# Column-tiled projections, router products and scores, and padded FFN weights, in a two-layer transformer kernel

## The chip, the core and the metric

The kernel runs on one core of a Trainium2 chip. A core has five engines with queues of their own: TensorE (matrix products; the profile splits it into PE, the products, and PEld, the loads of the stationary operand), VectorE (DVE), ScalarE (ACT), GpSimd (POOL) and SyncE (SP), which here issues DMAs. The metric is the device time of one execution in microseconds, lower is better. The unit of work is one call on a batch of 8 sequences of 512 tokens, each token 512 wide, in fp32.

## What is computed

The reference chains two post-norm layers. Cut to what matters here:

```python
# layer 0: 16 heads of 32, causal; then 8 experts, the best 2 of each token
x = layernorm(x + attn0(x))            # q, k, v = x @ W.T + b; softmax(q k^T / sqrt(32)) v; out @ WO.T + b
x = layernorm(x + moe(x))              # softmax router with LoRA, top 2, gate-up, silu, down, LoRA on both
# layer 1: 8 query heads of 64, 2 key/value heads, no mask; then a quantised FFN
x = layernorm(x + attn1(x))            # h = norm_scale * x / (norm + eps) * split_scale; x + out @ Wo.T
x = layernorm(x + ffn(x))              # W = (wq - 128) * scale; silu(x Wg^T) * (x Wu^T), then @ Wd^T; hidden 1408
```

## The kernel before

The program is one pass over four stages. In the profiled execution layer 0 attention takes the first 700 us or so, the experts run to about 1133 us, layer 1 attention to 1677 us and the FFN to the end.

**Layer 0 attention** (`attention0`) works a batch (one sequence) at a time, and in it four groups of four heads. A group's queries and keys are kept transposed: 4 heads x 32 features on the 128 partitions, 512 tokens along the row. `query` (L1301) and `key` (L1313) make them as four accumulated products of 128 x 128 weights by 128 x 512 inputs; `value` (L1294) and `project` (L1321) are products of the same size. `scores` (L1386) multiplies, for a block of 128 keys, the four heads' keys by the queries from that block on. A head has 32 features, so each of the four products uses 32 rows of the array and all 128 columns, and each writes its own PSUM bank. Key blocks come in three units: block 0 (512 queries), blocks 1 and 3 (384 and 128), block 2 (256). ACT then takes the exponential, POOL masks the diagonal block (L1395), and `product` (L1410) multiplies the values of each head (32 columns) by the probabilities, into a quarter of the partitions each. `normalise` (L1425) sums the probabilities with a matrix of ones, 32 columns a head, and DVE inverts and multiplies.

`plan` fills the slots: a slot is one unit of scores, then the projections or router products that are due in it, then the `product` of the unit before, and in every third slot a `normalise`. In the middle of this stage the framework's scheduler sets the order on each engine; at its start, in the last half of the last batch and afterwards the order is that of the source (`in_order`).

**The router** (`Router`) works beside the attention of later batches: `logits` (L491), `choose` (L503: four products of 128 tokens by 8 experts), `dispatch` (L547 and L548: ranks of the tokens within each expert, by products with a triangle and with ones) and `enter` (L588: 16 bf16 products of one-hot rows that write the table of tokens of each expert). LoRA products (`delta`, L781: 16 rows by 128 columns) are merged into the experts' weights in the same stage.

**Layer 1 attention** (`Attention1`) is planned by hand for every engine. Its products go through `multiply` (L1600), which issues each of them as a pair of 64-column halves, except for some of batch 0. `score` (L1745) multiplies 64-row keys by queries for two heads at a time, with all 128 columns; `product` (L1767) and the sums (L1775) use 64 columns a head.

**The FFN** (`IntegerFfn`) splits inputs and hidden values into a high and a low fp32r half. Of each batch, `hidden` (L1152) makes 11 blocks of 128 hidden features: 8 products for the gate (ps_g) and 8 for the up part (ps_u) with the integer weights as the stationary operand, and `out` (L1168) 8 products of the hidden halves with the down weights as the moving operand. The weights are held in two tiles: the first 20 units (gate and up of blocks 0 to 9) in a pool `c_weights` that is opened before layer 1 attention, the other 13 (all down weights, and gate and up of block 10) in `d_weights`, opened with the FFN. The pool `c_weights` lies on the right side of the memory, below the rows of batches 2 to 7, so what is in it sets the byte at which its first tile starts.

The lines of before that the change touches most:

```python
def multiply(self, b, out, lhsT, rhs, c):                       # layer 1
    for m in (slice(0, self.HD), slice(self.HD, P)) if b else (slice(0, P),):
        self.nc.tensor.matmul(out[m], lhsT=lhsT[:, m], rhs=rhs, start=c == 0, stop=c == ND - 1)
```

Of the kernel before, what the change touches and what calls it, by code (L numbers as in the profile page):

```python
# [54 lines left out]
N_VEC = 16 + 2 * NHID  # L55

# [360 lines left out]
class Router:  # L417
# [76 lines left out]
    def choose(self, b, parts, ps):  # L494
# [7 lines left out]
        for t in range(NT):  # L502
            nc.tensor.matmul(ps[:, t, :], lhsT=parts[:, ts(t, P)], rhs=self.gather, start=True, stop=True)  # L503
# [39 lines left out]
    def dispatch(self, b, ps):  # L543

        nc, small = self.nc, self.small
        flat = "p t e -> p (t e)"
        nc.tensor.matmul(ps.rearrange(flat), lhsT=self.before, rhs=self.both.rearrange(flat), start=True, stop=False)  # L547
        nc.tensor.matmul(ps.rearrange(flat), lhsT=self.ones, rhs=self.earlier.rearrange(flat), start=False, stop=True)  # L548
        here = slice(NT * b, NT * (b + 1))
        parts = small.tile([P, TOP_K, NT], F32, name="parts")  # L550
        for k in range(TOP_K):
            for of_expert, out in ((ps, self.ranks[:, k, here]), (self.part, parts[:, k, :])):
                mine = small.tile([P, NT, E], F32, name="mine")
                nc.vector.tensor_tensor(mine, of_expert, self.hots[:, k, here, :], ALU.mult)
                nc.vector.tensor_reduce(out, mine, AX.X, ALU.add)
# [27 lines left out]
    def enter(self, ps, low, high, column):  # L583

        nc, n = self.nc, TOP_K * NT
        for h, part in enumerate((low, high)):
            for i in range(n):
                nc.tensor.matmul(ps[:, h, :], lhsT=part[:, i, :], rhs=column[:, i, :], start=i == 0, stop=i == n - 1)  # L588
        nc.vector.tensor_tensor(self.table, ps[:, 0, :], self.table, ALU.add)
        nc.vector.scalar_tensor_tensor(self.table, ps[:, 1, :], float(P), self.table, ALU.mult, ALU.add)  # L590
# [632 lines left out]
def attention0(env, guard, keep, routes, experts, dram, p_mm, tiles_ctx):  # L1223
# [8 lines left out]
    with ExitStack() as phase:  # L1232
# [57 lines left out]

        def value(b, t):
            ps = mm([P, D], "ps_v")
            for c in range(ND):
                nc.tensor.matmul(ps, lhsT=xts[b][:, c, ts(t, P)], rhs=wv[:, c, :], start=c == 0, stop=c == ND - 1)  # L1294
            vs[t] = own.tile([P, D], F32, tag=f"v{t}", name=f"v{t}")
            nc.vector.tensor_tensor(vs[t], ps, row[:, 0, :], ALU.add)

        def query(b, g):
            ps = mm([P, S], "ps_q")
            for c in range(ND):  # L1300
                nc.tensor.matmul(ps, lhsT=wq[:, g, ts(c, P)], rhs=xts[b][:, c, :], start=c == 0, stop=c == ND - 1)  # L1301
# [8 lines left out]
        def key(b, g):  # L1310
            ps = mm([P, S], "ps_k")
            for c in range(ND):
                nc.tensor.matmul(ps, lhsT=wk[:, g, ts(c, P)], rhs=xts[b][:, c, :], start=c == 0, stop=c == ND - 1)  # L1313
# [4 lines left out]
        def project(b, t):  # L1318
            ps = mm([P, D], "ps_o")
            for c in range(ND):  # L1320
                nc.tensor.matmul(ps, lhsT=aoTs[b][:, c, ts(t, P)], rhs=wo[:, c, :], start=c == 0, stop=c == ND - 1)  # L1321
# [40 lines left out]
        def choose(b):  # L1362
            router.choose(b, logits.pop(b), mm([P, NT, E], "ps_r"))

        def dispatch(b, mm=mm):
            router.dispatch(b, mm([P, NT, E], "ps_rank"))
# [8 lines left out]
        def enter(rows, mm=mm):  # L1375
            router.enter(mm([P, 2, E * E_TILES], "ps_table"), *rows)

        def scores(b, g, u):
# [3 lines left out]
            for kt in UNITS[u]:  # L1382
                w = S - P * kt
                for j in range(4):
                    hs = slice(HD * j, HD * (j + 1))
                    nc.tensor.matmul(sc[:, j, width : width + w], lhsT=k[hs, ts(kt, P)], rhs=q[hs, P * kt :],  # L1386
                                     start=True, stop=True)
# [157 lines left out]
        project(b, 0)  # L1545
        project(b, 1)
        rows = one_hot(b - 1, (2, 3))
        project(b, 2)
        project(b, 3)
        experts.load(7)  # L1550
        enter(rows)
# [8 lines left out]
        choose(b)  # L1560
        tiles.step()
        merge()
        dispatch(b, tiles.aside)
# [4 lines left out]
        enter(rows, tiles.aside)  # L1568
# [8 lines left out]
class Attention1:  # L1577
# [19 lines left out]
    def multiply(self, b, out, lhsT, rhs, c):  # L1597

        for m in (slice(0, self.HD), slice(self.HD, P)) if b else (slice(0, P),):
            self.nc.tensor.matmul(out[m], lhsT=lhsT[:, m], rhs=rhs, start=c == 0, stop=c == ND - 1)  # L1600
# [87 lines left out]
    def batches(self, work, p_sc, p_av, weights, split):  # L1688
# [51 lines left out]
        def score(b, g, kt):  # L1740
            st = state[b]
            sc = p_sc.tile([P, 2, S], F32, tag="sc", name="sc1")
            for j in range(2):
                hs = slice(HD * j, HD * (j + 1))
                nc.tensor.matmul(sc[:, j, :], lhsT=st["kT"][hs, ts(kt, P)], rhs=st["qT"][g][hs, :],  # L1745
                                 start=True, stop=True)
# [121 lines left out]
def usual_pass(tc, ins, held_out):  # L1868
    nc = tc.nc
    with ExitStack() as ctx:  # L1870
# [4 lines left out]
        with tc.tile_pool(name="a_mm", bufs=2, space=PSUM) as p_mm, ExitStack() as attn1_ctx:  # L1875
# [29 lines left out]
            weights.open(ctx.enter_context(tc.tile_pool(name="c_weights", bufs=1, side="right")), weights.FIRST)  # L1905
# [309 lines left out]
```

## Time and profile before

| What | us |
|---|---|
| median of 3 runs | 2182.87 (2181.64 to 2183.12) |
| the profiled execution | 2183.3 |
| its span, first instruction to last | 2181.6 |
| TensorE drawn busy (PE) | 2151.6, 99% of the span |
| VectorE busy | 1273.8, 58% |
| ScalarE busy | 627.5, 29% |
| GpSimd busy | 497.8, 23% |

The costliest TensorE groups, from the page's list of groups of instructions (busy time of the group, mean length of one instruction):

| group | instructions | busy us | mean ns |
|---|---|---|---|
| L1168 ps_f, FFN out | 672 | 170.3 | 393 |
| L1152 ps_g and ps_u, FFN hidden, four groups | 352 each | 138.6 to 139.0 each | 394 to 395 |
| L1745 layer 1 scores, 64 rows x 128 columns | 512 | 127.2 | 615 |
| L1301, L1313, L1294, L1321 layer 0 projections, 128 x 128 | 256 each | 115.9 to 120.7 each | 598 to 613 |

In the profile's lines a TensorE form such as 32*128 is rows*columns of the array that the stationary operand fills, and 128x512 is partitions x elements of the moving operand. An fp32 product of the source appears as two instructions. Lengths of single matmuls overlap[...]; the distance from one start to the next is what a matmul costs.

### The profile page before, as it was taken

The page shows a single profiled execution, that of the slowest core. Times are in us where ns is not written, and L with a number is a line of the kernel's source. Part 1 is how long each engine was busy: PE and PEld are TensorE (multiplying, and loading weights), DVE is VectorE, ACT ScalarE, POOL GpSimd, SP SyncE. Part 2 cuts the span into 40 slices and gives each one's busy share as a digit, 9 for nine tenths or more (in the row PEclk, how much of TensorE's full clock was granted, in tenths as well). Part 3 has the DMA queues.
Part 4 walks back from the last instruction along what each step waited for, and adds up shares of the span by engine and source line. Part 5 has one row for each costly group of instructions (what it writes and reads, how often), then busy time and mean ns, then how long its engine had stood idle before and what let it go on. Part 6 is the DMA issues. An engine that isn't in the chain of part 4 may idle for free. (4 is left out here: it accounts for less than half of the span.)

```text
span 2181.6 us, 25149 instructions
## 1 busy us (share of the span) xinstructions
PE 2151.6 (99%) x9694; PEld 1077.7 (49%) x9694; DVE 1273.8 (58%) x2042; ACT 627.5 (29%) x907; POOL 497.8 (23%) x489
## 2 busy tenths in 40 slices
PE   9999999999999999999999999999999999999997
PEld 3334444444444444444443333333334888888876
DVE  3557665675758543324316988889857644555443
ACT  2332323323223231122123333333332232222222
POOL 2332414324233442132015122231211000000000
PEclk9999999999999999999999999999999999999999
DMA  8030302303132328787644121331201311111000
GB/s 304 20 94 4 97 20 78 97 1 97 33 102 78 107 67 232 212 228 207 192 142 157 49 87 58 97 97 39 78 1 44 102 59 58 58 58 58 20 20 21
DMA packets 159971, 194.87 MB, mean 89 GB/s; under 512 B 61011, under 2 KB 101971, under 8 KB 157283
## 3 DMA queue, kind: packets, MB, share of 16 engines
q1 hardware_dynamic: 148560, 157.49, 23.5%
q0 software_dynamic: 10560, 34.61, 5.5%
q8 instruction: 79, 1.29, 0.2%
q10 hardware_dynamic: 722, 1.07, 0.1%
q14 instruction: 50, 0.40, 0.1%
HBM read 123.67 MB, written 69.47 MB: 89 GB/s over the span
## 5 line engine op out<-in xcount | busy, mean ns | idle before, releaser
L903 PE MATMUL ps_gu<-experts,xrT 128*128 128x512 f32 (+1 forms) x520 | 247.2, 598 | 0.0
L1390 ACT ACTIVATE p<-sc 128x2048 f32<-128x2048 f32 (+1 forms) x96 | 152.9, 1592 | 162.2 <-PE sc L1386 135.8
L1157 DVE SCALAR_TENSOR_TENSOR hT<-ps_u,vec,sg 128x512 f32<-128x512 f32 x88 | 65.6, 745 | 194.6 <-PE ps_u L1152 194.6
L1395 POOL TENSOR_SCALAR_AFFINE_SELECT p<-p 128x512 f32<-128x512 f32 x128 | 92.4, 734 | 360.3 <-ACT p L1390 316.8
L1168 PE MATMUL ps_f<-ffn_w,h_half 128*128 128x512 f32 x672 | 170.3, 393 | 0.6 <-issue 0.4
L1007 POOL TENSOR_TENSOR g_total<-g_total,r_inv 128x512 f32<-128x512 f32 x64 | 89.6, 1400 | 343.7 <-DVE r_inv L1778 272.2
L1418 DVE TENSOR_TENSOR p<-p 128x1536 f32<-128x1536 f32 (+2 forms) x96 | 131.1, 1365 | 46.0 <-POOL p L1395 41.0
L1748 ACT ACTIVATE p<-sc 128x1024 f32<-128x1024 f32 x128 | 124.0, 1021 | 100.4 <-PE sc L1745 95.9
L905 DVE TENSOR_TENSOR h<-ps_gu,h 128x256 f32<-128x256 f32 x67 | 28.4, 424 | 208.8 <-ACT h L904 208.8
L1778 DVE RECIPROCAL r_inv<-r_inv 128x512 f32<-128x512 f32 x32 | 107.1, 3346 | 69.3 <-ACT r_inv L1004 69.3
L1168 PEld LDWEIGHTS ps_f<-ffn_w,h_half 128*128 128x128 f32 x672 | 124.3, 188 | 33.1 <-DVE h_half L1163 5.6
L903 PEld LDWEIGHTS ps_gu<-experts,xrT 128*128 128x128 f32 x520 | 95.8, 196 | 89.3 <-issue 89.0
L1152 PE MATMUL ps_g<-x_high,ffn_w 128*128 128x512 f32 x352 | 138.8, 394 | 0.9 <-DVE x L1719 0.9
L1152 PE MATMUL ps_g<-x_low,ffn_w 128*128 128x512 f32 x352 | 139.0, 395 | 0.0
L1152 PE MATMUL ps_u<-x_low,ffn_w 128*128 128x512 f32 x352 | 138.7, 394 | 0.0
L1152 PE MATMUL ps_u<-x_high,ffn_w 128*128 128x512 f32 x352 | 138.6, 394 | 0.0
L919 PE MATMUL ps_y<-experts,hT 128*128 128x512 f32 (+1 forms) x272 | 128.0, 593 | 0.5 <-ACT hT L913 0.5
L1745 PE MATMUL sc<-qT,kT 64*128 64x512 f32 x512 | 127.2, 615 | 1.0 <-ACT qT L1653 0.7
L1301 PE MATMUL ps_q<-experts 128*128 128x512 f32 x256 | 120.7, 613 | 4.8 <-DMA experts<-in_xT 4.5
L1767 PE MATMUL av<-p,v 128*64 128x512 f32 x512 | 120.9, 593 | 0.0
L1313 PE MATMUL ps_k<-experts 128*128 128x512 f32 x256 | 117.5, 602 | 0.0
L1600 PE MATMUL ps_o<-attn_out,aoT 128*64 128x512 f32 x512 | 116.4, 598 | 0.8 <-ACT r_inv L1004 0.8
(267 smaller groups left out, 3359.6 us busy)
## 6 DMA issues: line engine op xcount, KB each, us to landing
results<-y SPq DMA_DIRECT2D x68, 256.0 KB, 2.2
turned<-turned SPq DMA_DIRECT2D x56, 256.0 KB, 4.1
pair<-xrT SPq DMA_DIRECT2D x25, 512.0 KB, 2.9
xrT<-pair SPq DMA_DIRECT2D x100, 128.0 KB, 4.3
x<-in_x SPq DMA_DIRECT2D x8, 1024.0 KB, 8.5
experts<-in_gate_up SPq DMA_DIRECT2D x8, 1024.0 KB, 11.0
rows<-x SPq DMA_DIRECT2D x32, 256.0 KB, 2.3
x<-rows SPq DMA_DIRECT2D x8, 1024.0 KB, 16.2
```

The costliest lines, as they stand in the source:

```text
L903: nc.tensor.matmul(ps, lhsT=xT[:, c, :], rhs=self.weights(i, c), start=c == 0, stop=c == ND - 1)
L919: self.nc.tensor.matmul(ps, lhsT=hT[:, c, :], rhs=self.weights(i, ND + c), start=c == 0, stop=c == self.NI - 1)
L1152: nc.tensor.matmul(ps, lhsT=w[:, ts(dc, P)], rhs=x[:, dc, :], start=(dc, i) == (0, 0), stop=(dc, i) == (ND - 1, 1))
L1168: self.nc.tensor.matmul(os[t], lhsT=h[:, ts(t, P)], rhs=self.weights(2 * NHID + c), start=(c, i) == (0, 0), stop=(c, i) == (NHID - 1, 1))
L1301: nc.tensor.matmul(ps, lhsT=wq[:, g, ts(c, P)], rhs=xts[b][:, c, :], start=c == 0, stop=c == ND - 1)
L1313: nc.tensor.matmul(ps, lhsT=wk[:, g, ts(c, P)], rhs=xts[b][:, c, :], start=c == 0, stop=c == ND - 1)
L1390: nc.scalar.activation(p, sc[:, :, :width], AF.Exp, scale=scale)
L1418: nc.vector.tensor_tensor(total[:, :, P * kt :], total[:, :, P * kt :], p[:, :, at : at + w], ALU.add)
L1600: self.nc.tensor.matmul(out[m], lhsT=lhsT[:, m], rhs=rhs, start=c == 0, stop=c == ND - 1)
L1745: nc.tensor.matmul(sc[:, j, :], lhsT=st["kT"][hs, ts(kt, P)], rhs=st["qT"][g][hs, :], start=True, stop=True)
L1748: nc.scalar.activation(p, sc, AF.Exp, scale=scale)
L1767: nc.tensor.matmul(st["av"][HD * j : HD * (j + 1), :], lhsT=st["v"][:, kt, HD * j : HD * (j + 1)], rhs=p[:, j, :], start=kt == 0, stop=kt ...
```

## The change

A helper `matmul_by_columns` issues one product as several, each for a slice of the stationary operand's columns and the same slice of the output's partitions. It is used with

- 32 columns for all projections of layer 0 (`value`, `query`, `key`, `project`), except the output projections of the last batch, which come after the head loop and stay whole;
- 32 columns (`HD`) for the router products `choose`, `dispatch` and `enter`, except those that fall after the head loop, which are called with 128;
- 64 columns for the scores of both attention layers, two products for each head and key block;
- layer 1's `multiply`, whose slices are the same as before.

Besides, the pool `c_weights` gets a second tile of 56 floats, `c_aligned`, that nothing writes or reads.

```diff
+def matmul_by_columns(nc, out, lhsT, rhs, start=True, stop=True, columns=32):
+
+    for at in range(0, P, columns):
+        m = slice(at, at + columns)
+        nc.tensor.matmul(out[m], lhsT=lhsT[:, m], rhs=rhs, start=start, stop=stop)
...
         for t in range(NT):
-            nc.tensor.matmul(ps[:, t, :], lhsT=parts[:, ts(t, P)], rhs=self.gather, start=True, stop=True)
+            matmul_by_columns(nc, ps[:, t, :], parts[:, ts(t, P)], self.gather, columns=columns)
...
-        nc.tensor.matmul(ps.rearrange(flat), lhsT=self.before, rhs=self.both.rearrange(flat), start=True, stop=False)
-        nc.tensor.matmul(ps.rearrange(flat), lhsT=self.ones, rhs=self.earlier.rearrange(flat), start=False, stop=True)
+        out = ps.rearrange(flat)
+        matmul_by_columns(nc, out, self.before, self.both.rearrange(flat), stop=False, columns=columns)
+        matmul_by_columns(nc, out, self.ones, self.earlier.rearrange(flat), start=False, columns=columns)
...
-                nc.tensor.matmul(ps[:, h, :], lhsT=part[:, i, :], rhs=column[:, i, :], start=i == 0, stop=i == n - 1)
+                matmul_by_columns(nc, ps[:, h, :], part[:, i, :], column[:, i, :], i == 0, i == n - 1, columns)
...
+        def multiply(out, lhsT, rhs, c):
+            matmul_by_columns(nc, out, lhsT, rhs, start=c == 0, stop=c == ND - 1)
+
...
-                nc.tensor.matmul(ps, lhsT=wq[:, g, ts(c, P)], rhs=xts[b][:, c, :], start=c == 0, stop=c == ND - 1)
+                multiply(ps, wq[:, g, ts(c, P)], xts[b][:, c, :], c)
...
-        def project(b, t):
+        def wide(out, lhsT, rhs, c):
+            nc.tensor.matmul(out, lhsT=lhsT, rhs=rhs, start=c == 0, stop=c == ND - 1)
+
+        def project(b, t, out_of_heads=False):
...
-                nc.tensor.matmul(ps, lhsT=aoTs[b][:, c, ts(t, P)], rhs=wo[:, c, :], start=c == 0, stop=c == ND - 1)
+                (wide if out_of_heads else multiply)(ps, aoTs[b][:, c, ts(t, P)], wo[:, c, :], c)
...
-                    nc.tensor.matmul(sc[:, j, width : width + w], lhsT=k[hs, ts(kt, P)], rhs=q[hs, P * kt :],
-                                     start=True, stop=True)
+                    matmul_by_columns(nc, sc[:, j, width : width + w], k[hs, ts(kt, P)], q[hs, P * kt :], columns=64)
...
-                nc.tensor.matmul(sc[:, j, :], lhsT=st["kT"][hs, ts(kt, P)], rhs=st["qT"][g][hs, :],
-                                 start=True, stop=True)
+                matmul_by_columns(nc, sc[:, j, :], st["kT"][hs, ts(kt, P)], st["qT"][g][hs, :], columns=HD)
...
-            weights.open(ctx.enter_context(tc.tile_pool(name="c_weights", bufs=1, side="right")), weights.FIRST)
+            pool = ctx.enter_context(tc.tile_pool(name="c_weights", bufs=1, side="right"))
+            weights.open(pool, weights.FIRST)
+            pool.tile([P, 56], F32, name="c_aligned")
```

`value` and `key` change as `query` does. In layer 1, HD is 64.

More of the change, by code (lines that the diff above doesn't have):

```diff
@@ L492, in logits, with choose @@
                                   start=True, stop=True)
-    def choose(self, b, parts, ps):
+    def choose(self, b, parts, ps, columns):
         nc, small = self.nc, self.small
@@ L541, in choose, with dispatch @@
         nc.vector.tensor_tensor(self.carry, self.earlier[:, NT - 1, :], self.both[:, NT - 1, :], ALU.add)
-    def dispatch(self, b, ps):
+    def dispatch(self, b, ps, columns):
         nc, small = self.nc, self.small
         flat = "p t e -> p (t e)"
-        nc.tensor.matmul(ps.rearrange(flat), lhsT=self.before, rhs=self.both.rearrange(flat), start=True, stop=False)
-        nc.tensor.matmul(ps.rearrange(flat), lhsT=self.ones, rhs=self.earlier.rearrange(flat), start=False, stop=True)
+        out = ps.rearrange(flat)
+        matmul_by_columns(nc, out, self.before, self.both.rearrange(flat), stop=False, columns=columns)
+        matmul_by_columns(nc, out, self.ones, self.earlier.rearrange(flat), start=False, columns=columns)
         here = slice(NT * b, NT * (b + 1))
@@ L581, in one_hot, with enter @@
         return low, high, column
-    def enter(self, ps, low, high, column):
+    def enter(self, ps, low, high, column, columns):
         nc, n = self.nc, TOP_K * NT
@@ L1293, in value @@
             for c in range(ND):
-                nc.tensor.matmul(ps, lhsT=xts[b][:, c, ts(t, P)], rhs=wv[:, c, :], start=c == 0, stop=c == ND - 1)
+                multiply(ps, xts[b][:, c, ts(t, P)], wv[:, c, :], c)
             vs[t] = own.tile([P, D], F32, tag=f"v{t}", name=f"v{t}")
@@ L1312, in key @@
             for c in range(ND):
-                nc.tensor.matmul(ps, lhsT=wk[:, g, ts(c, P)], rhs=xts[b][:, c, :], start=c == 0, stop=c == ND - 1)
+                multiply(ps, wk[:, g, ts(c, P)], xts[b][:, c, :], c)
             k = own.tile([P, S], F32, tag="k", name="k", bufs=2)
@@ L1360, in score, with choose, dispatch @@
                 nc.scalar.copy(logits[b], ps)
[L1362 to L1366, printed above, removed]
+        def choose(b, columns=HD):
+            router.choose(b, logits.pop(b), mm([P, NT, E], "ps_r"), columns)
+        def dispatch(b, mm=mm, columns=HD):
+            router.dispatch(b, mm([P, NT, E], "ps_rank"), columns)
         rooms = {}
@@ L1373, in one_hot, with enter @@
             return router.one_hot(b, rooms[b], places)
-        def enter(rows, mm=mm):
-            router.enter(mm([P, 2, E * E_TILES], "ps_table"), *rows)
+        def enter(rows, mm=mm, columns=HD):
+            router.enter(mm([P, 2, E * E_TILES], "ps_table"), *rows, columns)
         def scores(b, g, u):
@@ L1544, in attention0 @@
         one_hot(b - 1, (0, 1))
-        project(b, 0)
-        project(b, 1)
+        project(b, 0, True)
+        project(b, 1, True)
         rows = one_hot(b - 1, (2, 3))
-        project(b, 2)
-        project(b, 3)
+        project(b, 2, True)
+        project(b, 3, True)
         experts.load(7)
-        enter(rows)
+        enter(rows, columns=P)
         for _ in range(2):
@@ L1559, in attention0 @@
         merge()
-        choose(b)
+        choose(b, P)
         tiles.step()
         merge()
-        dispatch(b, tiles.aside)
+        dispatch(b, tiles.aside, P)
         for places in ((0, 1), (2, 3)):
@@ L1567, in attention0 @@
             merge()
-        enter(rows, tiles.aside)
+        enter(rows, tiles.aside, P)
         tiles.of_fixed = router.fixed(routes)
@@ L1597, in multiply @@
     def multiply(self, b, out, lhsT, rhs, c):
-        for m in (slice(0, self.HD), slice(self.HD, P)) if b else (slice(0, P),):
-            self.nc.tensor.matmul(out[m], lhsT=lhsT[:, m], rhs=rhs, start=c == 0, stop=c == ND - 1)
+        matmul_by_columns(self.nc, out, lhsT, rhs, c == 0, c == ND - 1, self.HD if b else P)
     def prepare(self, b):
```

## The prediction

> **What bounds the kernel now.** I read the head of the page first, then the table of waits of the TensorE queue, then the engines' busy time by stage, then the TensorE timeline of each stage that the diff touches. Head and waits (the longest of all TensorE waits in total):
>
> ```profile
> span 2181.6 us, 25149 instructions
> PE 2151.6 (99%) x9694; PEld 1077.7 (49%) x9694; DVE 1273.8 (58%) x2042; ACT 627.5 (29%) x907; POOL 497.8 (23%) x489
> ```
>
> ```profile
> PE ps_q L1301 <- DMA experts<-in_xT: 4.5, 1, 4.5
> ```
>
> TensorE is never idle for long, so the time is TensorE's time, stage after stage. By stage (one batch of layer 0 attention, one of layer 1 attention, the integer FFN):
>
> ```profile
> core 0: us, PE busy (x) PEld busy (x) DVE busy (x) ACT busy (x) POOL busy (x), PEclk, DMA share, GB/s
> 437.70:527.10 89.40, 89.11 (x468) 37.53 (x464) 59.68 (x113) 27.89 (x32) 30.79 (x28) 1.00 0.19 60
> 1394.10:1462.20 68.10, 68.10 (x356) 24.39 (x354) 57.26 (x67) 21.77 (x30) 17.73 (x17) 1.00 0.25 78
> 1677.00:2170.00 493.00, 491.99 (x2114) 394.19 (x2114) 243.19 (x407) 130.49 (x205) 10.37 (x18) 1.00 0.16 53
> ```
>
> The next engine, VectorE, is busy 59.7 of 89.4, 57.3 of 68.1 and 243 of 493 us, so what TensorE saves is saved, up to some 10 us a batch. But busy is a bad measure of TensorE: a 512-column fp32 matmul is drawn 592 ns long while the next starts after 430. The differences of starts tell where its time goes. Layer 0, in three stretches:
>
> ```profile
> 300.69 1.06 PE L1410 MATMUL av<-p,v 128*32 128x512 f32 x8
> 301.57 1.04 PE L1425 MATMUL rs<-p,ones 128*32 128x512 f32 x8
> 302.54 0.71 PE L1386 MATMUL sc<-q,k 32*128 32x256 f32 x8
> 303.19 3.70 PE L1313 MATMUL ps_k<-experts 128*128 128x512 f32 x8
> 306.72 3.60 PE L1321 MATMUL ps_o<-experts,aoT 128*128 128x512 f32 x8
> 310.16 1.91 PE L588 MATMUL ps_table<-one_hot 128*128 128x256 bf16 x16
> ```
>
> ```profile
> 177.41 0.95 PE L503 MATMUL ps_r<-r_gather,logits 128*128 128x8 f32 x8
> 178.30 0.64 PE L1410 MATMUL av<-p,v 128*32 128x256 f32 x8
> ```
>
> Each fp32 matmul of the source is two instructions. ps_o takes 3.44 us for 8, so 0.430 us a step. av and rs use a quarter of the array (128*32), four run side by side, and 8 of them are two steps, 0.86. Against these: av 0.88 (+0.02 after a change of shape), rs 0.97 (+0.11 before one), sc 0.65 against two half steps of 0.215 (+0.22, a change on each side), ps_k 3.53 against 3.44 (+0.09 after one), ps_o +0 (same shape on both sides). So **a change of tile shape** costs about 0.105 us to empty the array, plus the exposed weight load: 0.10 to 0.11 into 128 columns, 0.02 to 0.03 into 32. It happens between 32*128 and 128*128 too, so the row count alone is enough. Layer 1:
>
> ```profile
> 1299.96 1.99 PE L1745 MATMUL sc<-qT,kT 64*128 64x512 f32 x8
> 1301.88 3.65 PE L1600 MATMUL ps_o<-attn_out,aoT 128*64 128x512 f32 x16
> 1305.37 1.89 PE L1767 MATMUL av<-p,v 128*64 128x512 f32 x8
> 1307.18 1.99 PE L1745 MATMUL sc<-qT,kT 64*128 64x512 f32 x8
> 1309.10 3.23 PE L1600 MATMUL ps_k<-hT,attn_qkv 128*64 128x512 f32 x14
> ```
>
> sc: 1.92 against 4 steps, 1.72: +0.20. ps_o in pairs of 64 columns: 3.49 against 8 steps, 3.44: +0.05, so splitting the same product by columns costs nothing in steady state. av: 1.81 against 1.72, +0.09 on leaving. FFN, an ordinary hidden block and the last one (block 10) of a batch:
>
> ```profile
> 1894.41 0.39 PE L1152 MATMUL ps_g<-x_high,ffn_w 128*128 128x512 f32 x1
> ...
> 1898.13 1.98 PE L1168 MATMUL ps_f<-ffn_w,h_half 128*128 128x512 f32 x8
> ```
>
> ```profile
> 1916.59 0.39 PE L1152 MATMUL ps_g<-x_high,ffn_w 128*128 128x512 f32 x1
> ...
> 1920.21 1.98 PE L1168 MATMUL ps_f<-ffn_w,h_half 128*128 128x512 f32 x8
> ```
>
> Both hold 16 matmuls: 3.72 us (232 ns each) and 3.62 us (226 ns each).
>
> **What the Trainium skill says.** "TensorEngine Tiling (Array Packing)", Key Properties: changing the tiling mode drains the engine, and different tiles load and multiply in parallel. The trace agrees, at about 0.105 us a drain. "TensorE: Matmul & The Clock Gate", LDWEIGHTS: a load takes columns / 1.2 ns whatever the rows, which gives 107, 53 and 27 ns for 128, 64 and 32 columns; the exposed 0.10 to 0.11, 0.05 and 0.02 to 0.03 us above agree. The same page, Part 3 (Packing small matmuls), states that row and column tiling compose, 16 tiles giving 10.6 times. No run here shows that: before splits rows or columns, never both. No page I found gives a speed for operand alignment.
>
> **The change, part by part.** I counted shape changes in the issue order of both programs. The order of work is the same (ACT and SP identical, DVE and POOL differ in a few swaps), apart from one thing named below.
>
> *Layer 0 attention.* With 32-column projections and router products, everything but the scores and the LoRA products has the shape of av and rs; the scores become 32*64. Changes of shape fall from 285 (190 into 128 columns, 95 into 32) to 216 (17 into 128, 96 into 64, 103 into 32). Before: 285 x 0.105 + 190 x 0.107 + 95 x 0.027 = 52.8 us. After: 216 x 0.105 + 17 x 0.107 + 96 x 0.053 + 103 x 0.027 = 32.4. Gain 20.4 us (2.6 in a middle batch, where 36 changes become 27). Bounds: if the eight loads of a score group go in two turns, 96 x 0.053 = 5.1 less; 22 if a drain costs 0.125 instead of 0.105 (69 fewer). The multiplication time is taken as unchanged: four 128*32 tiles already run at 0.430 us a step in rs, and two that read the same moving operand do so in ps_o of layer 1.
>
> *Three interrupted queries.* In batch 0 the scheduler puts score products inside a query three times. Before that fell after 2 of 4 matmuls; now after 5 of 16, where one tile runs alone and three stand idle. One more pair of steps each: 3 x 0.86 = 2.6 us lost (0 to 2.6).
>
> *Router products.* ps_r takes 0.89 us for 8 products of 8 columns, about 112 ns each: the load of 128 columns. As 32 small ones, loads of 27 ns in four tiles side by side, 8 rounds of about 34 ns make 0.27. In 7 of 8 batches: 7 x 0.6 = 4.3 us. The rank products (4 loads of 112 ns) give perhaps 7 x 0.2. I take 5.0, bounds 0 (issue of four times the instructions eats it) and 6.5. The table products (ps_table, bf16, 16 x 107 ns) stay bound by streaming: 64 in 16 rounds, nothing.
>
> *Layer 1 scores.* 64*64 instead of 64*128: still two shape changes per group, but the load on entry shrinks from 107 to 53 ns. 63 entries: 3.4 us. Bounds 0 (loads not parallel) and 3.4; the drain stays, since rows still change.
>
> *Padding.* The 56 floats push the first 20 weight units (ffn_w, hidden blocks 0 to 9) from byte 138720 of the partition to 138496, from 32 bytes off a 64-byte boundary onto one. Block 10's weights start at 92416, already on one, and block 10 is the fast one. 8 batches x 10 blocks x 0.10 us = 8.0 us. Bounds 0 (block 10 is fast for another reason: but blocks 4 and 5, with no extra work beside them, run at 232 too) and 8.5.
>
> The instructions of the scores and projections double and quadruple; they cost nothing as long as pairs of load and matmul issue faster than steps need them (av starts four within about 20 ns). DVE's 59.7 us a batch hides below TensorE's predicted 86.
>
> Sum: 20.4 - 2.6 + 5.0 + 3.4 + 8.0 = 34.2. The profiled execution took 2183.3 (span 2181.6), 0.4 above the median shown; 2183.3 - 34.2 - 0.4 = **2149** us on the median's footing.
>
> **Rivals.**
> *The padding does nothing* (0.09): 2157. For it: no page states the effect; against: block 10.
> *Split loads do not run in parallel in 2D tiles* (0.07): 8.5 back, 2157. Against: four row tiles load together, and so do four column tiles.
> *New waits in layer 0* (0.04): scores have one PSUM buffer, so the next group waits for ACT's exponentials (1.59 us mean); slots without a projection have little besides. If half of the layer 0 gain goes this way, 2160. Against: TensorE now waits 2.0 us for p in all.
> *Slower: row and column tiles together do not overlap* (0.05). If the two 64-column halves of a score run one after the other, the score time doubles: layer 0, 1280 columns a head group at 0.858 us per 512, 2.14 x 32 = 68.6 us; layer 1, 1.72 x 64 = 110. 2149 + 179 = 2328. It decides the sign once a fifth of that (34 of 179) is lost. For it: nothing in the trace shows 2D tiles; against: the skill's 16 tiles.
>
> **How the numbers follow.** 0.75 for the forecast. About 0.2% (4.4 us) is what this measurement tells from no change. Unknown costs at their ends give 2142 (22, 6.5, 3.4, 8.5, no loss) and 2170 (15.3 less 2.6, the rest nothing); all ends at once are unlikely, but each of them was read at 10 ns, so I add a little below: the range is 2140 to 2165, which takes in the three milder rivals. Faster 0.94, same 0.01, slower 0.05.
>
> **What would show it.** Layer 0 middle batches near 86 us instead of 89.4; no gap between projection, av and rs; a score group of 512 columns still two steps of 0.43; ps_r near 0.3; layer 1 batches 67.7 instead of 68.1; all FFN blocks at 226 ns. Wrong if score groups take twice their steps, if 32-column steps exceed 0.430, or if blocks 0 to 9 stay at 232.

## The result and the profile after

| What | before | changed |
|---|---|---|
| median of 4 runs each, us | 2182.67 (2181.64 to 2183.12) | 2156.64 (2156.18 to 2158.07) |
| ratio changed to before | | 0.9883, 95% interval 0.9867 to 0.9898 |
| span of the profiled execution, us | 2181.6 | 2156.4 |

The change takes 26.0 us off; the forecast was 34. First the head of the changed kernel's page, which gives the span and each engine's busy time:

```profile
span 2156.4 us, 35260 instructions
PE 2121.3 (98%) x14746; PEld 996.3 (46%) x14746; DVE 1280.0 (59%) x2042; ACT 628.8 (29%) x907; POOL 495.0 (23%) x489
```

TensorE has 5052 more products to issue (14746 in place of 9694) and is drawn busy 30 us less. The longest entries of its table of waits (total us, times, longest):

```profile
PE ps_q L62 <- DMA experts<-in_xT: 4.6, 1, 4.6
PE ps_logits L498 <- ACT scaled L800: 2.6, 6, 0.4
PE sc L62 <- ACT p L1403: 2.5, 1, 2.5
PE ps_f L1176 <- DVE h_half L1171: 2.0, 7, 0.5
PE ps_x1T L1361 <- DVE g_routed L605: 1.6, 1, 1.6
```

The first is as long as before (4.5), and ps_logits (1.7 before) and sc (2.0 before, in two waits) have grown a little. Two are new in the main: before, ps_f waited for h_half once, 0.2 us, and ps_x1T for g_routed not at all. By stage (starts of the first score, the first expert product, layer 1's first score and the FFN's first product in both traces):

| Stage | before | changed | difference |
|---|---|---|---|
| up to the first score | 14.7 | 15.0 | +0.3 |
| layer 0 attention | 687.5 | 673.6 | -13.9 |
| experts | 430.9 | 428.7 | -2.2 |
| layer 1 attention | 544.2 | 540.9 | -3.3 |
| FFN to the end of the span | 504.4 | 498.2 | -6.1 |

The same three windows as before the change, engine by engine: a middle batch of layer 0, one of layer 1, the FFN.

```profile
340.40:427.20 86.80, 86.22 (x1064) 28.27 (x1060) 59.36 (x113) 27.98 (x31) 29.55 (x27) 1.00 0.20 62
1376.30:1444.10 67.80, 67.80 (x422) 23.01 (x420) 57.30 (x67) 21.79 (x30) 17.73 (x17) 1.00 0.25 78
1658.00:2145.00 487.00, 483.73 (x2114) 394.66 (x2114) 243.24 (x409) 130.44 (x205) 10.65 (x18) 1.00 0.17 54
```

The layer 0 batch of this window takes 86.8 in place of 89.4 (forecast 86.0; batches 2, 3 and 6 take 86.5 to 86.6, batch 5 takes 87.8), a layer 1 batch 67.8 in place of 68.1 (67.7), the FFN's products 487 in place of 493 (485). Now the TensorE timeline of the same stretch of layer 0 (start, drawn length, line, output and inputs, rows*columns, count):

```profile
294.08 1.04 PE L1423 MATMUL av<-p,v 128*32 128x512 f32 x8
294.96 1.06 PE L1438 MATMUL rs<-p,ones 128*32 128x512 f32 x8
295.96 0.69 PE L62 MATMUL sc<-q,k 32*64 32x256 f32 x16
296.57 3.64 PE L62 MATMUL ps_k<-experts 128*32 128x512 f32 x32
300.03 3.62 PE L62 MATMUL ps_o<-experts,aoT 128*32 128x512 f32 x32
```

Starts subtracted: ps_k 3.46 where it was 3.53 (what is left is the shorter load on entry), and sc 0.617 where it was 0.644. The score group is the first surprise: two changes remain, and the shorter load should have saved 54 ns, not 27. The router and layer 1 in the same way:

```profile
175.19 0.44 PE L62 MATMUL ps_r<-r_gather,logits 128*32 128x8 f32 x31
...
175.48 0.65 PE L1423 MATMUL av<-p,v 128*32 128x256 f32 x7
```

```profile
1282.59 1.95 PE L62 MATMUL sc<-qT,kT 64*64 64x512 f32 x16
1284.47 3.65 PE L62 MATMUL ps_o<-attn_out,aoT 128*64 128x512 f32 x16
```

ps_r takes 0.28 us (0.89 before, forecast 0.27). A score group of layer 1 takes 1.88 (1.92 before; the forecast's 0.054 would give 1.87).

### The profile page after: what moved, and what is told of

It is laid out like the page before. It is cut to its first block, busy times and chain, and to the rows that moved or that the text cites. A ratio compares the mean times of both kernels' runs of the same rounds, so it can differ in the third digit from the quotient of the medians.

```text
span 2156.4 us, 35260 instructions
## 1 busy us (share of the span) xinstructions
PE 2121.3 (98%) x14746; PEld 996.3 (46%) x14746; DVE 1280.0 (59%) x2042; ACT 628.8 (29%) x907; POOL 495.0 (23%) x489
## 5 line engine op out<-in xcount | busy, mean ns | idle before, releaser
L1431 DVE TENSOR_TENSOR p<-p 128x1536 f32<-128x1536 f32 (+2 forms) x96 | 139.3, 1451 | 44.6 <-POOL p L1408 41.2
L62 PE MATMUL ps_q<-experts 128*32 128x512 f32 x1024 | 121.9, 605 | 4.9 <-DMA experts<-in_xT 4.6
L62 PE MATMUL sc<-qT,kT 64*64 64x512 f32 x1024 | 124.7, 602 | 1.1 <-ACT qT L1664 0.7
L62 PE MATMUL ps_k<-experts 128*32 128x512 f32 x1024 | 116.3, 594 | 0.0
## 6 DMA issues: line engine op xcount, KB each, us to landing
experts<-in_gate_up SPq DMA_DIRECT2D x8, 1024.0 KB, 11.4
```

The source lines that it names most:

```text
L62: nc.tensor.matmul(out[m], lhsT=lhsT[:, m], rhs=rhs, start=start, stop=stop)
L1431: nc.vector.tensor_tensor(total[:, :, P * kt :], total[:, :, P * kt :], p[:, :, at : at + w], ALU.add)
```

## The experiments

Each ran beside the kernel before; the medians of before lay between 2181.8 and 2182.9. Experiments 1 and 2 do one part of the change alone; the others start from the changed kernel.

### 1. The padding alone

```diff
-            weights.open(ctx.enter_context(tc.tile_pool(name="c_weights", bufs=1, side="right")), weights.FIRST)
+            pool = ctx.enter_context(tc.tile_pool(name="c_weights", bufs=1, side="right"))
+            weights.open(pool, weights.FIRST)
+            pool.tile([P, 56], F32, name="c_aligned")
```

> The kernel before with the padding alone (the FFN's weight tiles begin 224 bytes lower and nothing else changes). If the place of the weight tile sets the pace of its matmuls, blocks 0 to 9 of the FFN fall from 232-235 to about 227 ns a matmul, as in the changed kernel, and from 5.55 to about 5.44 us a block (80 blocks, 8.7 us); less the waits of ps_f for h_half that appeared at each batch's start, the time falls by 6 to 8 us. If those waits belong to the padding and not to the rest of the change, they show here too (7 of them, about 2 us). Rival: the FFN's gain of 6 us comes from the earlier stages (a different order or buffers), and the padding alone gives 0 to 1 us.

Measured: 2176.98 against 2182.63, ratio 0.9969 (0.9957 to 0.9982), so -5.7 us. FFN blocks 0 to 9 went from 5.55 to 5.44 us, products from 230 to 235 ns apart to 226 to 227, and the stage from its first product to its last from 492.6 to 486.5 us (486.4 in the changed kernel). The new wait is there too:

```profile
PE ps_f L1168 <- DVE h_half L1163: 2.0, 7, 0.5
```

So the FFN's whole gain is the padding's, and so is what is lost again at the start of each batch.

### 2. Layer 1's scores alone

```diff
-                nc.tensor.matmul(sc[:, j, :], lhsT=st["kT"][hs, ts(kt, P)], rhs=st["qT"][g][hs, :],
-                                 start=True, stop=True)
+                for m in (slice(0, HD), slice(HD, P)):
+                    nc.tensor.matmul(sc[m, j, :], lhsT=st["kT"][hs, kt * P + m.start : kt * P + m.stop],
+                                     rhs=st["qT"][g][hs, :], start=True, stop=True)
```

> The kernel before with only layer 1's score products issued as pairs of 64 columns. Forecast's term: 63 entries of 54 ns, -3.4 us. Theory after the result (a group now starts four tiles, each 6.7 ns behind the one before, instead of two): 40 ns an entry, group excess 171 in place of 211 ns, -2.5 us, layer 1 batches 67.8 in place of 68.1 us. Rival (the 3.2 us that layer 1 lost in the changed kernel came from what layer 0 left behind, for example other buffers or loads): 0.

Measured: 2180.76, ratio 0.9992 (0.9984 to 1.0001). The timing can't tell it from no change; the stage can: 542.1 us in place of 544.2, batches 67.8 in place of 68.1, a score group's surplus over its four steps 171 ns in place of 211. The gain is 40 ns an entry, not 54. In the changed kernel layer 1 lost 3.3; the other microsecond is in its first batch (55.7 us in place of 56.7; 56.8 here), and that batch varies from 55.3 to 56.8 us among runs with the same scores.

### 3 and 4. Layer 0's scores in 128 and in 32 columns

```diff
-                    matmul_by_columns(nc, sc[:, j, width : width + w], k[hs, ts(kt, P)], q[hs, P * kt :], columns=64)
+                    matmul_by_columns(nc, sc[:, j, width : width + w], k[hs, ts(kt, P)], q[hs, P * kt :], columns=P)
```

and the same with `columns=HD` (32).

> The changed kernel with layer 0's scores issued as whole 128 columns again (8 tiles of 32*64 become 4 of 32*128 in each group of four heads). Every score group is still entered from 32-column work and left to it. Theory (the exposed load of the first tile and the lag of the tiles both count): entry load +54 ns, lag of the tiles -27 ns, so +27 ns x 96 groups = +2.6 us against the changed kernel. Forecast's reading (load alone): +54 ns x 96 = +5.2 us. Rival (scores of 64 columns bring nothing in a layer of 32 columns): 0 or a gain.

> The changed kernel with layer 0's scores in 32 columns, as the projections are: sixteen tiles of 32*32 in each group of four heads. Theory (drain for every change of tile shape in rows or columns, load of the first tile, lag of the tiles): load -27 ns, lag of 16 tiles in place of 8 +54 ns, drain unchanged since the rows differ: +27 ns x 96 = about +2.6 us against the changed kernel. Rival A (load alone counts): -27 ns x 96 = -2.6 us. Rival B (only a change of column width drains, so sharing the 32 columns does away with it): -0.1 us or more x 192 changes = -15 us or more.

Measured: 2159.68 with 128 columns and 2170.93 with 32, against 2156.64 with 64. The same group of 256 queries, in the timelines of the runs with 128 and with 32 columns:

```profile
295.99 0.71 PE L62 MATMUL sc<-q,k 32*128 32x256 f32 x8
296.63 3.64 PE L62 MATMUL ps_k<-experts 128*32 128x512 f32 x32
```

```profile
301.81 0.73 PE L62 MATMUL sc<-q,k 32*32 32x256 f32 x32
302.47 3.64 PE L62 MATMUL ps_k<-experts 128*32 128x512 f32 x32
```

Start to start 0.64 and 0.66 us, and 0.62 for 64 columns: the width in the middle is the quickest. The starts of the single products of these three groups, in ns from the group's first, say why (an fp32 product is two passes, so each tile appears in two rounds):

```
columns   tiles   second round starts   its last tile starts   next product starts
128         4            320                    340                    644
 64         8            266                    313                    617
 32        16            240                    356                    660
```

The second round starts after 213 ns of streaming and the load of the tile, 107, 53 and 27 ns. Its last tile starts 20, 47 and 116 ns after its first, 6.7 ns a tile up to the fourteenth and 13 to 17 for the last two. The next product starts 304 ns after that last tile in all three, 91 more than it streams, so the drain is the same whether four, eight or sixteen tiles are open, and sharing the width of 32 columns with the projections doesn't save it (rival B of experiment 4 falls). Load and **lag of the tiles** pull against each other: 64 columns save 54 ns of load and give back 27 of lag, 32 columns save 27 more and give back 69.

With 32 columns it gets worse where key blocks 1 and 3 come together, as the second one has 128 queries only:

```profile
291.66 1.50 PE L62 MATMUL sc<-q,k 32*32 32x384 f32 x64
293.08 3.64 PE L62 MATMUL ps_q<-experts 128*32 128x512 f32 x32
```

1.42 us, 1.05 with 64 columns. The second of the products of 128 queries starts 185 ns after the first (why, the trace doesn't show), and from there a round moves on by about 16 ns a tile, so its sixteen need some 250 ns, while 128 columns stream in half of the 213 ns that 256 take. 32 such groups at 0.37 us and 64 others at about 0.04 make 14.4 us, and layer 0 went from 673.6 to 686.3 (700.2 less 13.9). I had not expected this. The sum of experiment 3 (+2.6) shows in the groups (surplus 217 to 225 ns in place of 190 to 196) but not in layer 0 as a whole (673.4 us): a wait of 1.2 us described below was absent, and in six batches slot 3.2 is 0.14 us shorter in place of 0.03 longer, as its ps_lora starts 0.54 us after scores of 32*128 and 0.62 us after those of 32*64. So the median's +3.0 agrees with the +2.6 by luck: in the profile layer 0 is 0.2 us shorter, and the experts' stage 1.9 us longer, where TensorE's clock was halved for longer (see **Experts** in the part on the prediction).

### 5 and 6. Two other pads

```diff
-            pool.tile([P, 56], F32, name="c_aligned")
+            pool.tile([P, 8], F32, name="c_aligned")
```

and the same with 24 floats.

> The changed kernel with a pad of 8 floats in place of 56: the FFN's first weight tile then starts at byte 138688 of a partition, a multiple of 64 but not of 128 (before: 138720, a multiple of 32 alone; changed: 138496, a multiple of 256). Theory 64 (a 32-byte offset inside a 64-byte line is what costs): FFN blocks 0 to 9 stay at 5.44 us and about 227 ns a matmul, time as the changed kernel's. Rival 128 or 256 (a larger line): blocks go back to 5.55 us and 232-235 ns, +6 us.

> The changed kernel with a pad of 24 floats: the FFN's first weight tile starts at byte 138624, a multiple of 128 but not of 256. Reading of the pad of 8 (a multiple of 64 alone: blocks 5.49 us, half of the gain). If the line is 128 bytes: 5.44 us as in the changed kernel. If it is 256 bytes or more: 5.46 to 5.49 us, +1 to +3 us.

Measured:

| pad, floats | first weight tile at byte | a multiple of | FFN block, us | FFN, first product to last, us | median |
|---|---|---|---|---|---|
| none (before) | 138720 | 32 | 5.55 | 492.6 | 2182.67 |
| 8 | 138688 | 64 | 5.49 | 489.5 | 2162.85 |
| 24 | 138624 | 128 | 5.54 and 5.59 in turn | 493.3 | 2164.58 |
| 56 | 138496 | 256 | 5.44 | 486.4 | 2156.64 |

The medians of the pads of 8, 24 and 56 differ by the pad alone; that of "none" lacks the rest of the change too. Block 10, whose tile stays at 92416, a multiple of 256, had its 16 products 226 to 227 ns apart in all four.

The pad of 24 is as slow as none, though it is better aligned than the pad of 8. Neither reading holds: what counts isn't the largest power of two that divides the address up to 128. A line of 256 bytes, or the distance of the weights from something else that is read at the same time, both fit the four points; no run tells them apart, and the cause stays open.

### 7. Queries of batch 0 a slot earlier

```diff
-                    todo[g, 0 if by_dma and ng == 0 else 1].append(lambda nb=nb, ng=ng: query(nb, ng))
+                    todo[g, 0 if by_dma and ng == 0 or b == 0 and g else 1].append(lambda nb=nb, ng=ng: query(nb, ng))
```

> The changed kernel with batch 0's queries of heads groups 2 to 4 and of the next batch placed one slot earlier, so that the scheduler no longer cuts them in two around a score group (5 + 11 products). Theory (each cut query costs about one more change of shape and one more round of loads and lag, and leaves one tile ahead of the others; forecast +2.6 us for three, trace about 0.5 each): batch 0 shortens by 1 to 2.5 us. Rival (batch 0 is bound by the loads of weights and inputs and by ACT, not by the products): 0.

Measured: 2158.89, batch 0 unchanged (68.1 us). But the kernel wasn't what I meant to run: the scheduler now cut the keys. The changed kernel, then this one:

```profile
42.91 1.88 PE L62 MATMUL ps_q<-experts 128*32 128x512 f32 x10
44.72 1.12 PE L62 MATMUL sc<-q,k 32*64 32x384 f32 x32
45.77 2.35 PE L62 MATMUL ps_q<-experts 128*32 128x512 f32 x19
```

```profile
63.46 1.02 PE L62 MATMUL ps_k<-experts 128*32 128x512 f32 x2
64.41 0.69 PE L62 MATMUL sc<-q,k 32*64 32x256 f32 x16
65.03 3.20 PE L62 MATMUL ps_k<-experts 128*32 128x512 f32 x27
```

Ten instructions are five products: one round of four tiles and one more product, alone. In the second listing the cut comes after two instructions, which is one product: it holds TensorE for 0.95 us up to the scores, and the other 15 follow. So the run says nothing of the rival.

### 8. Batch 0 with no product cut

Queries of batch 0 a slot earlier by the line of experiment 7, its keys too, and TensorE in source order to the end of that batch:

```diff
-                    todo[g, 1 if by_dma and ng == 0 else 2].append(lambda nb=nb, ng=ng: key(nb, ng))
+                    todo[g, 1 if by_dma and ng == 0 or b == 0 and g else 2].append(lambda nb=nb, ng=ng: key(nb, ng))
...
-                    begun.close()
+                    if b:
+                        begun.close()
```

> The changed kernel with batch 0's queries and keys a slot earlier and TensorE in the order of the source through batch 0, so that no product of 32 columns is cut by a score group (in the run with early queries the scheduler cut the keys 1 + 15 in place of the queries 5 + 11, and the time stayed). Theory (a cut that isn't at a multiple of four leaves a round in which one tile works and three stand idle, one pass of 0.43 us for each cut, and takes the lead of that tile along until the next drain): the three head groups of batch 0 shorten by 0.4 to 0.6 us each, batch 0 from 68.0 to 66.5 us. Rival (batch 0 is bound by ScalarE's exponentials): 68 us or more.

Measured: 2155.79, which the medians can't tell from the changed kernel's; the stage can: batch 0 took 66.6 us in place of 68.0, as the theory had it. The three head groups shortened by 0.46, 0.31 and 0.60 us; new waits for ScalarE's exponentials before two score groups took 0.18 each. So the cuts do cost: 0.3 to 0.6 us each, net of what the new order brings.

### 9 and 10. Where the LoRA merges stand

Experiment 9 puts both merges of a middle batch behind the slot's attention products (`late`); experiment 10 leaves one there and moves the other from slot 3.2 to 0.2 (slot 3.2 is head group 3, unit 2, both counted from 0). The edit of experiment 10 (in experiment 9 the last line has `late[3, 2]` in place of `late[0, 2]`):

```diff
-                    todo[2, 2 if by_dma else 1].append(merge)
-                    todo[3, 2 if by_dma else 1].insert(0, merge)
+                    (late if by_dma else todo)[2, 2 if by_dma else 1].append(merge)
+                    (late[0, 2] if by_dma else todo[3, 1]).insert(0, merge)
```

> The changed kernel with the two LoRA merges of each middle batch placed after the slot's attention products instead of before them. Theory (in these two slots TensorE waits for ScalarE to empty one of the two PSUM buffers, about 1.3 us a slot of which the changes of shape are no part, which is why they gained nothing from the 32-column tiles): ps_lora then finds its buffers free, the wait of 1.3 us goes from most of the 12 slots, 8 to 15 us less, middle batches near 84.5 us. Rival A (the slots are bound by the throughput of ScalarE and GpSimd, which have the same work): 0 to -2 us. Rival B (the exponentials come later behind the merges, and the next slot waits instead): 0 or slower.

> The changed kernel with one LoRA merge of each middle batch moved behind the products of its slot 2.2 (as in the run with both merges late) and the other taken out of slot 3.2 and put behind the products of slot 0.2. Reading of the run with both late: slot 2.2 and the one after it gave 0.63 us a batch; slot 3.2 gave 0.8 and the values of the next batch, which then waited for ScalarE to empty the merge's PSUM buffers, took back 1.1. Theory (a merge costs nothing only where the next product that needs a PSUM buffer comes late): 0.63 in 2.2, 1.4 less in 3.2, 0.4 to 0.8 more in 0.2, so 1.2 to 1.6 us for each of 6 batches, -7 to -10 us. Rival (throughput of ScalarE and GpSimd): no more than -2 us.

Measured: 2156.89 (both late: no gain) and 2150.21 (one moved: 6.4 us less, a little under what was expected). In the changed kernel ps_lora holds TensorE 1.93 us for four instructions. They are two products: behind av the second one starts 15 ns after the first and the group takes 1.06; here it starts 0.88 us after it, when ScalarE has emptied the buffer of ps_k. The changed kernel, then experiment 9:

```profile
321.76 2.00 PE L789 MATMUL ps_lora<-lora 16*128 16x512 f32 x4
323.69 1.07 PE L1423 MATMUL av<-p,v 128*32 128x384 f32 x16
```

```profile
322.02 1.14 PE L789 MATMUL ps_lora<-lora 16*128 16x512 f32 x4
323.08 1.11 PE L62 MATMUL sc<-q,k 32*64 32x512 f32 x16
...
344.28 1.07 PE L62 MATMUL ps_v<-experts 128*32 128x512 f32 x8 [1.02 <-ACT scaled L800]
```

The last line is the price: the merge of slot 3.2 holds both buffers, ScalarE empties them only in turn, and the next batch's second block of values waits 1.02 us. Slot 2.2 gave 1.00 and the next took 0.37; slot 3.2 gave 0.6 to 0.8 in four of six batches, and the next took 0.9 to 1.2 in five. Rival B of experiment 9 holds for one of the two merges. With that merge in slot 0.2, whose next buffer is wanted late, slot 0.2 costs 1.05 more, slot 3.2 1.6 to 1.9 less in five of six batches, and layer 0 takes 663.8 us in place of 673.6. Of these 9.8 us, 1.2 are the wait in batch 5 that is described below, and 1.5 lie in the last batch, where TensorE's clock is the cause (see the last batch, in the part on the prediction). So the merges are limited by when the two PSUM buffers come free, not by ScalarE's throughput.

One sentence of my expectation doesn't stand: that these slots "gained nothing from the 32-column tiles" because they wait. Counting their changes of shape again by the forecast's own prices gives -0.13 us for slot 2.2 and +0.16 for slot 3.2, whose ps_lora used to follow scores of the same shape; measured were -0.06 and +0.14. They are slow for another reason, and that reason is no part of the miss.

### 11. The FFN's normalisation later

```diff
-            env.layernorm(b, env.ins.out[b])
+            self.norm = env.layernorm(b, env.ins.out[b], later=True)
...
                 self.blocks(b + 1, c)
+            if c == 2 and b:
+                self.norm()
```

with `later`, `layernorm` returns its four last multiplications and stores as a function.

> The changed kernel with the FFN's normalisation of a finished batch (four multiplications on VectorE and the stores of the result) issued after the hidden values of the next batch's third block, so that h_half does not queue behind them. Theory (the padding's gain of 0.11 us in 80 blocks, 8.7 us, lost 2.0 to 2.5 us again in 7 waits of ps_f for h_half at the start of a batch): the third block falls from 3.51 to about 3.2 us in six or seven batches, -2 us. Rival (the matmuls themselves gave less; the wait moves on to the next block because VectorE has the same work): 0.

Measured: 2155.14, FFN from first product to last 482.5 us in place of 486.4. VectorE at the start of a batch in the changed kernel:

```profile
1790.42 1.92 DVE L192 TENSOR_SCALAR x<-x,mv,rstd 128x512 f32<-128x512 f32 x4 [0.83 <-POOL rstd L190]
1792.25 1.29 DVE L1171 TENSOR_TENSOR h_half<-hT,h_half 128x512 fp32r<-128x512 f32 x2
```

The multiplications wait 0.83 us for GpSimd's rstd and stand ahead of h_half, for which ps_f waits. With the edit no wait of ps_f for h_half is left. The gain of 3.9 us is twice the 2.0 us of the waits that the table shows. The starts have the rest: once in each of batches 2 to 6 the waiting ps_f starts 640 to 666 ns after the product before it, where 227 is the pace, and the product after it 335 to 341 ns after that, so a wait costs 0.52 to 0.55 us. The table counts 0.25 to 0.28 of it, since it starts to count when the product before has been drawn to its end, 389 ns after its start.

### 12. The three edits that helped, together

The edits of experiments 8, 10 and 11 on the changed kernel.

> The changed kernel with the three edits that shortened a stage: the FFN's normalisation issued later, the merges moved to slots 2.2 and 0.2, and batch 0 uncut. If the three lie in different stages and add up: FFN -3 to -4 us (486.5 us from its first product to its last becomes about 483), middle batches 85.1 us in place of 86.6, batch 0 66.7 in place of 68.0, together -10 to -14 us against the changed kernel: 2143 to 2147 us. Rival (what is gained in layer 0 is waited for at its end, where the first tiles of the experts need loads and GpSimd): layer 0 gives less than 8 us, total 2149 us or more.

Measured: 2143.86 (2142.12 to 2146.7), ratio to before 0.9825 (0.9812 to 0.9838); the changed kernel's was 0.9883. Its windows of a middle batch of layer 0, the FFN and batch 0:

```profile
335.50:420.60 85.10, 84.81 (x1065) 27.80 (x1061) 60.96 (x113) 28.00 (x31) 30.63 (x28) 1.00 0.21 64
1650.70:2133.30 482.60, 481.92 (x2114) 394.88 (x2114) 243.36 (x406) 130.49 (x205) 10.35 (x17) 1.00 0.17 54
14.60:81.10 66.50, 65.98 (x792) 20.92 (x792) 31.65 (x24) 23.86 (x22) 24.90 (x19) 1.00 0.61 202
```

Together they take 12.8 us off the changed kernel, as forecast, though alone their medians gave 0.9, 6.4 and 1.5. By stage, the FFN and batch 0 gain what they gained alone. Layer 0 as a whole does not: 664.0 us, and 663.8 with the merges alone, since its last batch took 87.1 us in place of 85.5, again for the clock.

## Why the prediction was right, and where its sum was off

The direction held, and so did the mechanism of each term but the padding's, whose reason fell; the sum was 8 us too large. Term by term:

| Term of the forecast | forecast | measured |
|---|---|---|
| layer 0, changes of shape | -20.4 | about -11 (the stage's -13.9 less the next two) |
| three interrupted queries | +2.6 | about +2.1 |
| router products | -5.0 | about -4.8 |
| layer 1 scores | -3.4 | -2.1 alone |
| padding | -8.0 | -6.1 |

**Changes of shape** is the term that was mis-sized. Three things went into it.

First, "the exposed weight load" was priced right and the start of the tiles was not priced at all. The forecast said that instructions "cost nothing as long as pairs of load and matmul issue faster than steps need them". They do need nothing in steady state, but at a change the drain begins only when the last tile has ended, and every tile starts 6.7 ns behind the one before. That is 27 ns in 96 groups, 2.6 us, and 14 ns in 63 entries of layer 1. The Trainium skill has this in "TensorE: Matmul & The Clock Gate", Part 3 (Packing small matmuls): the span of a pack is one matmul plus about 4 ns for each further tile. I used that page for the load and not for this; the trace puts it at 6.7. The price of 0.105 us a change also mixed two things: in both traces the next product starts some 90 to 96 ns after the last tile has streamed, and to this comes the lag of the tiles, 20 ns for four, 47 for eight and nothing for a whole 128x128 product. Before, 88 of the 285 changes left a whole product; after, 4 of 216 did. With drain and lag counted apart, this part of the gain is 3.6 us and not 7.2.

Second, the last batch. Its share of the sum is about -2.5 (34 changes become 29 with shorter loads, -1.7, and router products), but from its first score to the first expert product it grew by 1.2 us (85.8 to 86.9). I had noted that VectorE and GpSimd "differ in a few swaps" and cost that at nothing. One of the swaps is here. VectorE and TensorE before, then changed:

```profile
675.39 0.68 DVE L1418 TENSOR_TENSOR p<-p 128x512 f32<-128x512 f32 x1
...
676.32 0.14 DVE L597 TENSOR_REDUCE g_routed<-ps_count 128x1 f32<-128x4 f32 x1
...
676.52 1.09 PE L1347 MATMUL ps_x1T<-ident,x 128*128 128x128 f32 x8
```

```profile
659.52 2.01 DVE L1431 TENSOR_TENSOR p<-p 128x512 f32<-128x512 f32 x2
...
661.78 0.15 DVE L605 TENSOR_REDUCE g_routed<-ps_count 128x1 f32<-128x4 f32 x1
661.98 1.09 PE L1361 MATMUL ps_x1T<-ident,x 128*128 128x128 f32 x8 [1.57 <-DVE g_routed L605]
```

Before, VectorE read ps_count between the two additions to p; changed, after both. ps_x1T needs that buffer, and TensorE stands 1.57 us. (`in_order` fixes the order of TensorE alone here; VectorE's is the scheduler's.) All eleven runs with the changed layer 0 have this order and a wait of 1.5 to 1.6 us; that the order causes it is read from the traces, no run isolates it. Later in this batch a score group waits 2.48 us for the exponentials of the one before (1.76 before the change).

The rest is TensorE's clock. The products behind that score group, before and changed, and the window of the changed kernel in which they lie, with one of the experts' stage of before:

```profile
697.28 1.06 PE L1410 MATMUL av<-p,v 128*32 128x512 f32 x8
698.28 1.09 PE L878 MATMUL ps_xrT<-ident,first_rows 128*128 128x128 f32 x8
```

```profile
682.30 1.94 PE L1423 MATMUL av<-p,v 128*32 128x512 f32 x8
684.17 1.74 PE L886 MATMUL ps_xrT<-ident,first_rows 128*128 128x128 f32 x8
```

```profile
682.12:685.53 3.41, 3.41 (x31) 1.57 (x16) 1.73 (x13) 1.88 (x1) 1.08 (x2) 0.50 0.00 1
712.37:715.78 3.41, 3.41 (x5) 1.41 (x5) 3.38 (x4) 0.60 (x1) 3.21 (x4) 0.50 0.54 154
```

The number after the last bracket is the granted clock: 0.50 for 3.41 us, in which a second pass of av starts 835 ns after the first (433 at full clock) and products of ps_xrT are 213 ns apart (109). So slot 3.1 took 6.47 us in place of 5.10. Before, two such stretches lay in the experts' stage; now one lies there and one here. In experiment 10 it came after the end of layer 0, and the slot took 5.07 us, with the same wait for the exponentials in front of it; in the other nine it lies in this slot, which took 6.2 to 7.5. What decides where a stretch falls no run isolates. The wait for ps_count, the longer wait for the exponentials and the clock, 1.6, 0.7 and 1.4 us, are about the 3.7 us that this batch lacks.

Third, in batch 5 the values wait 1.2 us once for ScalarE's `scaled`, behind an addition on GpSimd that itself waits for a load. Experiments 3 and 4 don't have this wait and experiment 7 has 2.7 us of it in four waits, with the same merges and loads; so it seems to go by small shifts in time. Together these (3.6, 3.7 and 1.2) make some 8 of the 9 us; the rest I can't assign to one place.

**Interrupted queries.** Forecast 0.86 us each. The three slots grew by 0.63, 0.21 and 0.63 us where the slots around them shrank by 0.21 to 0.24: 0.85, 0.43 and 0.85. The middle one had a longer slot before, too (5.27 us, 4.85 the others). Experiment 8 supports the cause.

**Router products.** From first product to next group ps_r fell by 0.61 us, as the forecast had it, and the rank products by 0.33. But each of these groups holds one change of shape on leaving (0.13 at the forecast's price), which the first term had counted already. Without it they gave 0.48 and 0.20, 4.8 us in 7 batches. The forecast's 0.6 counted that change twice; its 5.0 came out because it took less than its own parts, 4.3 and 1.4.

**Padding.** The blocks gave a little more than was counted, 0.107 us in 80 blocks, 8.6 us. The loss of 2.5 us was not in the forecast: VectorE "243 of 493 us" busy looked free, but a batch's start has all of its normalisation at once, and there h_half comes late as TensorE becomes quicker. Experiments 1 and 11 show both halves. The reason given for the gain, "from 32 bytes off a 64-byte boundary onto one", fell in experiments 5 and 6: a pad that meets it gives half, and one that meets a stricter rule gives nothing. The guess from block 10 was right in size for this pad only.

**Experts.** Their -2.2 us was in no term. It is the clock again: in all fourteen profiles this stage, which no edit touches, took 428.7 to 429.1 us where it held 3.4 us of halved clock (as in the changed kernel) and 430.4 to 431.3 us where it held 6.8 (as before). So what the last batch lost to the clock (1.4 us) the experts more than gained: in the sum it nearly cancels, but by stage it makes layer 0 look worse, and the experts better, than the edits made them.

Of the rivals, "2D tiles do not overlap" and "split loads do not run in parallel" are out: eight tiles of 32*64 start within 47 ns, and their second round comes after one load of 53 ns. In the words of "TensorEngine Tiling (Array Packing)", Key Properties, "Different tiles can execute LdWeights and Matmul in parallel", which this trace now shows for tiles split both ways. "New waits" was right in kind, but the wait that it named, of scores for the exponentials, grew by 0.7 us only in the last batch, of its 11.4; the waits for g_routed and `scaled` (1.6 and 1.2 us) were others.

## What to carry to other kernels

Where small products share the array with large ones, count changes of tile shape and price each as drain, load of the first tile, and lag of the last tile; the narrowest tile isn't the cheapest, and streams too short for the issue of their tiles cost far more than the load they save. A product split into tiles must not be cut by a scheduler at other than a whole round. When TensorE gains in a stage, look at the instructions that stand at its edges (the start of a batch, the last batch, buffers that another engine empties): there a neighbour that is half idle on average is late, and a swap on its queue can cost more than the edit saves. And read the granted clock of a stage before a difference of a microsecond or two in it is put down to an edit.

## What was not expected of the hardware

- Tiles of a group start 6.7 ns apart (20 ns over 4, 47 over 8), and the last two of sixteen 13 to 17 ns apart.
- Emptying the array before a change costs the same for 4, 8 and 16 open tiles: the next product starts 304 ns after the last tile of a pass of 213 ns.
- The byte at which the FFN's weight tile starts changes the pace of its products from 226 to 232 ns and more, and not in the order of its alignment: 138496, 138688, 138720 and 138624 gave blocks of 5.44, 5.49, 5.55 and 5.54 to 5.59 us.
- On this single core TensorE's clock was halved for stretches of 3.4 or 6.8 us in the middle of the kernel, one to three times between 670 and 770 us of every profile, and a stretch moved from one stage to the next between kernels that differ little.
